# Attention scores from fp16 halves, one exponential per tile, and splits moved to GpSimd

## The chip, the core and the metric

The kernel runs on one core of one Trainium2 chip. A core has TensorE (PE), VectorE (DVE), ScalarE (ACT), GpSimd (POOL) and SyncE (SP), which each take their own instructions in order and meet through semaphores. The metric is the device time of one execution in microseconds; lower is better. Times of one instruction come from one profiled execution.

## What is computed

The reference is one transformer layer on 2048 tokens of width 256: a layer norm, attention with 16 heads of 128, an output projection, a layer norm and a residual; then a mixture of 8 small experts of which the router picks 2 per token, again with norms and a residual. The weights of attention are codes times a scale for each block of 32 rows. What matters here, cut:

```python
q = _mxfp4_matmul(x, wq_codes, wq_scales) + bq      # likewise k, v
scores = jnp.einsum('bqhd,bkhd->bhqk', q, k) / jnp.sqrt(jnp.float32(HEAD_DIM))
attn = jax.nn.softmax(scores, axis=-1)
out = jnp.einsum('bhqk,bkhd->bqhd', attn, v).reshape(B, S, NUM_HEADS * HEAD_DIM)
return _mxfp4_matmul(out, wo_codes, wo_scales) + bo
```

## The kernel before

The kernel keeps nearly fp32 precision by cutting numbers in two parts, a high and a low one, and multiplying high by high, high by low and low by high. Each product of 128 x 128 by 128 x 512 therefore costs three matmuls.

It has three stages: a prologue (layer norm of x, transposed and cut into two fp16 parts; the first weights; the first Q and K), the attention loop, and a tail (output projection, norms, router, experts). The instruction order is written by hand: the program fixes the order on each engine, and a tile layer only adds the semaphore waits that the use of tiles and buffers asks for.

The attention loop (L611 to L665) runs over 256 steps g; a step is one head h and one tile t of 128 queries against all 2048 keys. In a step, in program order:

- `scores_half` (L382) for keys 0 to 1023: six matmuls into a PSUM buffer of 128 x 1024 fp32 (L388, L389, L392), from Q and K held as two fp32r parts; then VectorE takes the row maximum (L393). The PSUM pool has three such buffers, each a tile of its own.
- `recip` of the step before (L413, L416), `flush` (which issues VectorE work left pending by the projections), and one `pv_unit`: six matmuls (L455 to L457) of probabilities times V, for a block of four tiles that lies 13 units back.
- `high_part` of the step before (L420): ScalarE scales the fp32 probabilities p to fp16 (ph), and SP issues a DMA that transposes ph into the tile PT.
- `scores_half` for keys 1024 to 2047, `negmax` (L399), and `softmax` (L406): two exponentials of 1024 columns, one for each half's buffer, each with a row sum.
- another `pv_unit`; then `low_part` of the step before: p times the reciprocal minus ph, 1536 columns on VectorE (L432) and 512 on GpSimd (L438, L439), and its DMA transpose (L440).
- `fill` (L472): a piece of the projections for coming steps, four matmuls of 512 columns (Q or K, L187) or of 256 (V, L206). ScalarE writes the high part (L193, L216), and VectorE the low part (L194, L217), both out of PSUM; the next piece uses the same PSUM buffer "pj".

After eight units a block's result leaves PSUM in two fp16 parts (L463 on ScalarE, L464 on VectorE) and goes to memory by a DMA from GpSimd's queue (L467). SP issues all transposes, in program order: high, low, high, low.

In the prologue V's weights are divided by a power of two found from their largest scale: a maximum on VectorE, an all-reduce over partitions on GpSimd (L341), and a few VectorE steps. Q's and K's weights have a fixed factor.

The lines that the exponential's structure rests on:

```python
s = psS.tile([128, 2, 512], F32, name="s")          # L385, pool of 3
nc.scalar.activation(                               # L406, for each half
    p[:, bass.ts(half, 1024)], ss[half].rearrange("p a b -> p (a b)"),
    AF.Exp, bias=m[:, 2:3], scale=ISQ, accum_out=m[:, 3 + half : 4 + half],
)
```

## Time and profile before

| | |
|---|---|
| time, three runs | 1897.87 us median (1895.89 to 1903.79) |
| the profiled execution: span | 1897.5 us |
| its mean granted TensorE clock | 0.994 |
| attention loop, first to last L399 | 42.4 to 1601.4 us |
| TensorE busy (matmul) | 1832.9 us, 97% |
| VectorE busy | 1640.9 us, 86% |
| ScalarE busy | 1328.2 us, 70% |
| GpSimd busy | 883.7 us, 47% |
| DMA transposes | 2 x 256, 4.0 to 4.1 us from issue to landing |

Times are microseconds from the span's start. PE is TensorE's matmul, PEld its weight load, which runs beside it. Matmuls are pipelined and their ends are modelled, so a busy TensorE is not a TensorE at its rate: the distance from one matmul's start to the next tells that. A group's row gives the line, the engine, the operation, what is written from what, the shape and the count; then busy us in total and mean ns of one; then the idle time of the engine ahead of it and what ended most of that. "issue" is waiting for which the profile shows no releaser.

### The profile page before, as it was taken

To read this page: it belongs to the slowest core of one execution; us is meant where nothing else is said; L and a number is where in the kernel's file an instruction comes from. 1 tells how busy PE (TensorE), PEld (TensorE's weight loads), DVE (VectorE), ACT (ScalarE), POOL (GpSimd) and SP (SyncE) were. 2 spreads that over 40 slices of the span, in tenths; PEclk is the share of its full clock that TensorE was granted. 3 is DMA by queue.
4 is the path that set the end of the run, shared out by engine and by line. 5 is a ranking of instruction groups with operands and counts; after the bars stand their busy time and mean duration, and the time that the engine had idled before them with its cause. 6 is when DMAs were issued, how large, how long until landed. Compare 5 with 4: busy or idle time off the path is not lost.

```text
span 1897.5 us, 25913 instructions
## 1 busy us (share of the span) xinstructions
PE 1832.9 (97%) x8886; PEld 1161.5 (61%) x8886; DVE 1640.9 (86%) x2293; ACT 1328.2 (70%) x1730; POOL 883.7 (47%) x732
## 2 busy tenths in 40 slices
PE   5899999999999999999999999999999999899998
PEld 3555556555565565655655556655556555588887
DVE  5999998999999999999999999999999987468566
ACT  4877788778787778787878788777878777123232
POOL 2853465445444554455445544554444565233222
PEclk8999999999999999999999999999999999999999
DMA  2999999999999998899989988999899999982121
GB/s 75 192 188 179 179 207 184 188 184 194 192 184 182 208 202 186 183 193 204 183 174 199 205 180 187 190 210 185 181 186 192 222 222 243 257 250 70 51 68 56
DMA packets 1147220, 342.20 MB, mean 180 GB/s; under 512 B 1077008, under 2 KB 1137328, under 8 KB 1147088
## 3 DMA queue, kind: packets, MB, share of 16 engines
q1 hardware_dynamic: 1139152, 321.57, 81.9%
q0 software_dynamic: 5216, 16.81, 3.7%
q10 hardware_dynamic: 2720, 2.17, 0.4%
q8 instruction: 70, 1.15, 0.3%
q14 instruction: 62, 0.51, 0.1%
HBM read 53.08 MB, written 18.94 MB: 38 GB/s over the span
## 4 chain that ended last, share of the span: by engine, by line
PE 48%; DVE 9%; ACT 4%; DMA 4%; issue 3%; SPq 1%; POOL 0%; ACTq 0%; DVEq 0%; POOLq 0%
PE s L389 6%; PE s L388 6%; PE s L392 6%; PE pv L455 6%; PE pv L456 6%; PE pv L457 6%; PE gup L845 5%; DVE pl L432 4%; DMA pt<-pl 3%; PE pj L187 3%; ACT ph L420 3%; DVE m L393 2%; PE dps L884 2%; PE pj L206 1%; PE op L690 1%
## 5 line engine op out<-in xcount | busy, mean ns | idle before, releaser
L420 ACT ACTIVATE ph<-p,m 128x2048 f16<-128x2048 f32 x256 | 512.6, 2003 | 240.3 <-issue 134.9
L393 DVE TENSOR_REDUCE m<-s 128x1 f32<-128x1024 f32 x512 | 623.2, 1217 | 60.9 <-PE s L392 58.1
L406 ACT ACTIVATE p<-s,m 128x1024 f32<-128x1024 f32 x512 | 565.3, 1110 | 80.6 <-DVE m L399 76.4
L432 DVE SCALAR_TENSOR_TENSOR pl<-p,m,ph 128x1536 f16<-128x1536 f32 (+1 forms) x256 | 575.8, 2249 | 47.1 <-ACT ph L420 21.1
L439 POOL TENSOR_TENSOR pl<-pr,ph 128x512 f16<-128x512 f32 x262 | 486.5, 1857 | 264.7 <-issue 142.2
L388 PE MATMUL s<-kT,qT 128*128 128x512 f32 x1024 | 485.1, 474 | 5.3 <-ACT p L406 5.3
L389 PE MATMUL s<-kT,qT 128*128 128x512 f32 x1024 | 403.8, 394 | 0.0
L455 PE MATMUL pv<-pt,v 128*128 128x512 f16 x1024 | 393.4, 384 | 2.2 <-DVE o L464 2.0
L456 PE MATMUL pv<-pt,v 128*128 128x512 f16 x1024 | 388.7, 380 | 2.9 <-DMA pt<-pl 1.7
L457 PE MATMUL pv<-pt,v 128*128 128x512 f16 x1024 | 388.6, 379 | 0.0
L438 POOL TENSOR_SCALAR pr<-p,m 128x512 f32<-128x512 f32 x262 | 187.3, 715 | 329.5 <-DVE m L416 307.1
L392 PE MATMUL s<-kT,qT 128*128 128x512 f32 x1024 | 317.2, 391 | 0.0
L388 PEld LDWEIGHTS s<-kT,qT 128*128 128x128 f32 x1024 | 193.3, 189 | 79.0 <-ACT p L406 10.1
L392 PEld LDWEIGHTS s<-kT,qT 128*128 128x128 f32 x1024 | 192.2, 188 | 45.1
L389 PEld LDWEIGHTS s<-kT,qT 128*128 128x128 f32 x1024 | 193.5, 189 | 33.3
L455 PEld LDWEIGHTS <-v 128*128 128x128 f16 x1024 | 99.4, 97 | 185.7 <-issue 116.5
L457 PEld LDWEIGHTS <-v 128*128 128x128 f16 x1024 | 100.3, 98 | 121.2 <-issue 1.5
L456 PEld LDWEIGHTS <-v 128*128 128x128 f16 x1024 | 101.2, 99 | 75.3 <-issue 4.7
L859 POOL TENSOR_TENSOR hh<-sg,hh 128x512 fp32r<-128x512 f32 x42 | 54.5, 1299 | 143.6 <-ACT hh L858 106.6
L467 POOL DMA_DIRECT2D ot_d<-o x63 | 37.2, 590 | 172.8 <-DVE o L464 172.7
L858 ACT CAST hh<-sg 128x512 fp32r<-128x512 f32 (+1 forms) x45 | 27.5, 611 | 116.0 <-DVE sg L870 115.9
L406 ACT ACTIVATION_READ_ACCUMULATOR p<-s,m 128x1 f32 x512 | 99.7, 195 | 0.0
(160 smaller groups left out, 1727.5 us busy)
## 6 DMA issues: line engine op xcount, KB each, us to landing
oi<-ot_d SPq DMA_DIRECT2D x32, 512.0 KB, 5.9
ot_d<-o POOLq DMA_DIRECT2D x63, 256.0 KB, 5.4
pt<-ph SPq DMA_TRANSPOSE x256, 4.1
pt<-pl SPq DMA_TRANSPOSE x256, 4.0
cu<-ct_d SPq DMA_DIRECT2D x16, 256.0 KB, 3.7
xt<-in_L_attn_x SPq DMA_DIRECT2D x4, 512.0 KB, 5.2
wos<-in_L_attn_wo_scales ACTq DMA_DIRECT2D x32, 64.0 KB, 4.2
woc<-in_L_attn_wo_codes SPq DMA_DIRECT2D x8, 256.0 KB, 3.4
```

The lines of the kernel that those rows point to most:

```text
L388: nc.tensor.matmul(s[:, j, :], q[:, 0, qc], k[:, 0, :], start=True, stop=False)
L389: nc.tensor.matmul(s[:, j, :], q[:, 0, qc], k[:, 1, :], start=False, stop=False)
L392: nc.tensor.matmul(s[:, j, :], q[:, 1, qc], k[:, 0, :], start=False, stop=True)
L393: nc.vector.tensor_reduce(m[:, half : half + 1], s.rearrange("p a b -> p (a b)"), AX.X, ALU.max)
L406: nc.scalar.activation(p[:, bass.ts(half, 1024)], ss[half].rearrange("p a b -> p (a b)"), AF.Exp, bias=m[:, 2:3], scale=ISQ, accum_out=m[: ...
L420: nc.scalar.activation(ph, p, AF.Copy, scale=m[:, 6:7])
L432: nc.vector.scalar_tensor_tensor(pl[:, :cv], p[:, :cv], m[:, 6:7], ph[:, :cv], ALU.mult, ALU.subtract)
L438: nc.gpsimd.tensor_scalar(pr, p[:, cs], m[:, 6:7], 1.0, ALU.mult, ALU.mult)
L439: nc.gpsimd.tensor_tensor(pl[:, cs], pr, ph[:, cs], ALU.subtract)
L455: nc.tensor.matmul(ps, vh, d[:, :, c, :], start=(c == 0), stop=False)
L456: nc.tensor.matmul(ps, vh, d[:, :, 16 + c, :], start=False, stop=False)
L457: nc.tensor.matmul(ps, vl, d[:, :, c, :], start=False, stop=(c == 15))
```

## The change

- **Scores.** Q and K become two fp16 parts in place of two fp32r parts. The weights of Q, K and V are each divided by a power of two found from the largest scale and bias; the product of the powers goes into the exponential's scale, which is now read from memory. The powers come from a chain of two PE transposes, one small matmul and VectorE steps in the prologue, in place of the all-reduce.
- **One exponential.** The three PSUM score buffers become one tile `s6` of three slots of 1024 columns. A tile's two halves take the next two slots, and one instruction makes the exponential over both; where the slots are 2 and 0 the halves are exchanged. A small ScalarE copy scales the row sum, and `recip` is one instruction.
- **Splits on GpSimd.** In the loop, ScalarE evacuates a projection's PSUM (Q, K and V) to an fp32 tile `t32`, and GpSimd makes both fp16 parts from it. The block results of P.V go the same way.
- **Low part on VectorE.** `low_part` becomes two calls of `low_half` of 1024 columns: the first at the end of the step in which `high_part` ran, the second a step later, after the next first reduce. The low part's transpose is issued with the second.
- **Prologue.** The start is put in another order around the new scales, and its PSUM tiles come from `s6` too. Buffers of the tail move (the tile `at`, the load of one block).

The core of the diff; prologue order, renamed operands and comments are cut:

```diff
     def scale_s(which):
-        f = sig[:, 1:2] if which == "v" else 1.0 / XS
+        f = sig[:, 2, IX[which] : IX[which] + 1]
         ps, sc, cd = raw[(0, which)]
...
-    psS = ctx.enter_context(tc.tile_pool(name="psS", bufs=3, space=PSUM))
     psA = ctx.enter_context(tc.tile_pool(name="psA", bufs=1, space=PSUM))
+    s6_ctx = ExitStack()
+    s6 = s6_ctx.enter_context(tc.tile_pool(name="ps6", bufs=1, space=PSUM)).tile(
+        [128, 3, 1024], F32, name="s"
+    )
+    slots = [0]
+
+    def s_slot():
+        slots[0] += 1
+        return (slots[0] - 1) % 3
+
+    def s_pair():
+        return s6[:, s_slot()].rearrange("p (a b) -> p a b", a=2)
+
...
     def proj_psum(tag):
         if tag == "s":
-            return psS.tile([128, 2, 512], F32, name="pjs", tag="s", bufs=3)[:, 0]
+            return s_pair()[:, 0]
...
-    def proj_qk(which, h, b, tag="pj"):
+    def proj_qk(which, h, b, tag="pj", wide=None):
         w = W[(h // 2, which)]
-        bias = (bqT if which == "q" else bkT)[:, h : h + 1]
+        bias = bqs[:, IX[which], h : h + 1]
...
-        t = kqv.tile([128, 2, 512], F32R, name=which + "T", bufs=8 if which == "k" else 2)
-        nc.scalar.activation(t[:, 0, :], ps, AF.Identity, bias=bias)
-        pending.append(lambda: nc.vector.scalar_tensor_tensor(
-            t[:, 1, :], ps, bias, t[:, 0, :].bitcast(F32), ALU.add, ALU.subtract
-        ))
+        t = kqv.tile([128, 2, 512], HP, name=which + "T", bufs=8 if which == "k" else 2)
+        if wide is None:
+            nc.scalar.activation(t[:, 0, :], ps, AF.Identity, bias=bias)
+            pending.append(lambda: nc.vector.scalar_tensor_tensor(
+                t[:, 1, :], ps, bias, t[:, 0, :], ALU.add, ALU.subtract
+            ))
+        else:
+            t32 = wide.tile([128, 512], F32, name="t32")
+            nc.scalar.activation(t32, ps, AF.Identity, bias=bias)
+            nc.gpsimd.tensor_copy(t[:, 0, :], t32)
+            nc.gpsimd.tensor_tensor(t[:, 1, :], t32, t[:, 0, :], ALU.subtract)
...
+        if wide is None:
+            nc.scalar.copy(v[:, 0, sl, :], psv)
+            pending.append(lambda: nc.vector.tensor_tensor(
+                v[:, 1, sl, :], psv, v[:, 0, sl, :], ALU.subtract
+            ))
+        else:
+            t32 = wide.tile([128, 512], F32, name="t32")[:, : n * 256].rearrange(
+                "p (t d) -> p t d", d=256
+            )
+            nc.scalar.copy(t32, psv)
+            nc.gpsimd.tensor_copy(v[:, 0, sl, :], t32)
+            nc.gpsimd.tensor_tensor(v[:, 1, sl, :], t32, v[:, 0, sl, :], ALU.subtract)
...
-        smax = st.tile([128, 128], F32, bufs=1)
+        smax = st.tile([128, 3, 128], F32, bufs=1)
+        b48 = st.tile([48, 128], F32, bufs=1)
...
+        for i, scales in enumerate((wq_scales, wk_scales, wv_scales)):
+            nc.scalar.dma_start(
+                out=smax[:, i], in_=scales.rearrange("b (c n) -> (b c) n", n=128)
+            )
+        for i, bias in enumerate((bq, bk, bv)):
+            nc.scalar.dma_start(
+                out=b48[16 * i : 16 * i + 16], in_=bias.rearrange("(h p) -> h p", p=128)
+            )
...
+        def sig_rows():
+            ps = psA.tile([128, 512], F32, name="smt", tag="pj")
+            nc.tensor.transpose(ps[:3, :128], sm[:, 0:3], ident)
+            sgp["t"] = ps
+
+        def sig_pow():
+            nc.vector.tensor_reduce(t3[:, 0:1], sgp["t"][:3, :128], AX.X, ALU.max)
+            nc.vector.tensor_scalar(t3[:, 1:2], t3[:, 0:1], 1e-30, None, ALU.max)
+            nc.vector.tensor_scalar(
+                t3.bitcast(I32)[:, 2:3], t3.bitcast(I32)[:, 1:2], 0x7F800000, None,
+                ALU.bitwise_and,
+            )
+            nc.vector.tensor_scalar(t3[:, 3:6], ident[:3, :3], t3[:, 2:3], None, ALU.mult)
+            ps = psA.tile([128, 512], F32, name="sgb", tag="pj")
+            nc.tensor.matmul(ps[:, :3], one3, t3[:, 3:6], start=True, stop=True)
+            sgp["s"] = ps
+
+        def sig_all():
+            nc.vector.tensor_scalar(sig[:, 0], sgp["s"][:, :3], 0.125, None, ALU.mult)
+            nc.vector.reciprocal(sig[:, 1], sig[:, 0])
+            nc.vector.tensor_scalar(sig[:, 2], sig[:, 1], 1.0 / XS, None, ALU.mult)
+
...

     def scores_half(h, t, half, m):
         q = Q[(h, t // 4)]
         qc = bass.ts(t % 4, 128)
-        s = psS.tile([128, 2, 512], F32, name="s")
+        slot = s_slot()
+        s = s6[:, slot].rearrange("p (a b) -> p a b", a=2)
         for j in range(2):
...
             nc.tensor.matmul(s[:, j, :], q[:, 1, qc], k[:, 0, :], start=False, stop=True)
-        nc.vector.tensor_reduce(
-            m[:, half : half + 1], s.rearrange("p a b -> p (a b)"), AX.X, ALU.max
-        )
-        return s
+        nc.vector.tensor_reduce(m[:, half : half + 1], s6[:, slot], AX.X, ALU.max)
+        return slot

     def negmax(m):
         nc.vector.tensor_scalar(
-            m[:, 2:3], m[:, 0:1], m[:, 1:2], -ISQ, ALU.max, ALU.mult
-        )
-
-    def softmax(h, t, ss, m):
+            m[:, 2:3], m[:, 0:1], m[:, 1:2], ssc[:, 1:2], ALU.max, ALU.mult
+        )
+
+    def softmax(slot0, slot1, m):
         p = soft.tile([128, S], F32, name="p")
-        for half in range(2):
-            nc.scalar.activation(
-                p[:, bass.ts(half, 1024)], ss[half].rearrange("p a b -> p (a b)"),
-                AF.Exp, bias=m[:, 2:3], scale=ISQ, accum_out=m[:, 3 + half : 4 + half],
-            )
+        src = s6[:, slot0 : slot1 + 1 : slot1 - slot0]
+        nc.scalar.activation(
+            p.rearrange("p (a b) -> p a b", a=2), src,
+            AF.Exp, bias=m[:, 2:3], scale=ssc[:, 0:1], accum_out=m[:, 3:4],
+        )
+        nc.scalar.activation(m[:, 4:5], m[:, 3:4], AF.Copy, scale=1.0 / PS)
         return p

     def recip(m):
-        nc.vector.tensor_scalar(
-            m[:, 5:6], m[:, 3:4], m[:, 4:5], 1.0 / PS, ALU.add, ALU.mult
-        )
-        nc.vector.reciprocal(m[:, 6:7], m[:, 5:6])
+        nc.vector.reciprocal(m[:, 6:7], m[:, 4:5])

     def high_part(h, t, m, p):
...
+        if half == 0:
+            LOW[(h, t)] = soft.tile([128, S], HP, name="pl")
+        pl = LOW[(h, t)]
+        cs = bass.ts(half, 1024)
         nc.vector.scalar_tensor_tensor(
-            pl[:, :cv], p[:, :cv], m[:, 6:7], ph[:, :cv], ALU.mult, ALU.subtract
-        )
-        for c in range(cv, S, POOL_COLS):
-            cs = slice(c, c + POOL_COLS)
-            pr = soft.tile([128, POOL_COLS], F32, name="pr", bufs=1)
-            nc.gpsimd.tensor_scalar(pr, p[:, cs], m[:, 6:7], 1.0, ALU.mult, ALU.mult)
-            nc.gpsimd.tensor_tensor(pl[:, cs], pr, ph[:, cs], ALU.subtract)
-        nc.sync.dma_start_transpose(
-            out=PT[(h, t // 4)][:, t % 4, 16:32, :], in_=pl
-        )
+            pl[:, cs], p[:, cs], m[:, 6:7], ph[:, cs], ALU.mult, ALU.subtract
+        )
+        if half == 1:
+            nc.sync.dma_start_transpose(
+                out=PT[(h, t // 4)][:, t % 4, 16:32, :], in_=LOW.pop((h, t))
+            )

     pvps = {}
...
@@ -458,12 +527,16 @@
         if c1 == 16:
             if (h, b) == (NH - 1, 3):
                 o = kqv.tile([128, 2, 512], HP, name="o_last", tag="v", bufs=7)
+                nc.scalar.activation(o[:, 0, :], ps, AF.Copy, scale=1.0 / PS)
+                nc.vector.scalar_tensor_tensor(
+                    o[:, 1, :], ps, 1.0 / PS, o[:, 0, :], ALU.mult, ALU.subtract
+                )
             else:
                 o = soft.tile([128, 2, 512], HP, name="o", bufs=1)
-            nc.scalar.activation(o[:, 0, :], ps, AF.Copy, scale=1.0 / PS)
-            nc.vector.scalar_tensor_tensor(
-                o[:, 1, :], ps, 1.0 / PS, o[:, 0, :], ALU.mult, ALU.subtract
-            )
+                t32 = soft.tile([128, 512], F32, name="t32")
+                nc.scalar.activation(t32, ps, AF.Copy, scale=1.0 / PS)
+                nc.gpsimd.tensor_copy(o[:, 0, :], t32)
+                nc.gpsimd.tensor_tensor(o[:, 1, :], t32, o[:, 0, :], ALU.subtract)
             nc.gpsimd.dma_start(out=ot_d[b][:, h], in_=o)
...
@@ -615,31 +687,36 @@
             if t in (0, 3, 6) and h % 2 == 0 and h + 2 < NH:
                 load_w(h // 2 + 1, "vkq"[t // 3], stage, nc.sync)
             m = small.tile([128, 8], F32, name="m", bufs=6)
-            s0 = scores_half(h, t, 0, m)
+            order = (1, 0) if slots[0] % 3 == 2 else (0, 1)
+            s0 = scores_half(h, t, order[0], m)
             if g == 0:
                 proj_v(0, 0, 2)
                 proj_v(0, 2, 2, "pv")
         if g == NS:
+            load_oi(0, 1, 1)
             load_oi(0, 1, 2)
             load_oi(0, 1, 3)
         if prev is not None:
             recip(prev[2])
+        if prev2 is not None:
+            low_half(1, *prev2)
+        if prev is not None:
+            prev = (*prev, high_part(*prev))
         flush()
         if defer:
             pv_unit(2 * g - 1)
             defer = False
         pv_unit(2 * g)
+        if live:
+            s1 = scores_half(h, t, order[1], m)
+            negmax(m)
+            p = softmax(min(s0, s1), max(s0, s1), m)
         if prev is not None:
-            hl = high_part(*prev)
-        if live:
-            s1 = scores_half(h, t, 1, m)
-            negmax(m)
-            p = softmax(h, t, (s0, s1), m)
+            low_half(0, *prev)
+        prev2 = prev
         first = live and (2 * g + 1 - PVLAG) % 8 == 0
         if not first:
             pv_unit(2 * g + 1)
-        if prev is not None:
-            low_part(*prev, hl)
         if live:
             fill(h, t)
...
     UEND = 2 * (NS + 2)
-
-    # -------------------------------------------------------------------- tail
+    s6_ctx.close()
+    psS = ctx.enter_context(tc.tile_pool(name="psS", bufs=3, space=PSUM))
```

## The prediction

> **What bounds the kernel now.** I read the page's busy shares first, then the stretch between the first and the last of the 256 steps, then a few steps row by row, then the groups by shape. The page:

> ```profile
> span 1897.5 us, 25913 instructions
> ## 1 busy us (share of the span) xinstructions
> PE 1832.9 (97%) x8886; PEld 1161.5 (61%) x8886; DVE 1640.9 (86%) x2293; ACT 1328.2 (70%) x1730; POOL 883.7 (47%) x732
> ```

> TensorE looks full and VectorE nearly so. L399 runs once a step; its view gives 256 starts from 42.4 to 1601.4 us, so a step takes 1559.0 / 255 = 6.11 us, and attention is 82% of the span. Its stretch (columns: busy us of each engine, granted clock, DMA share, GB/s):

> ```profile
> 42.40:1601.40 1559.00, 1531.53 (x7052) 916.60 (x7051) 1439.59 (x1827) 1235.39 (x1576) 787.80 (x647) 1.00 0.96 193
> ```

> Whether TensorE is at its rate is told by the distance between matmul starts (timeline: start us, us, engine, line):

> ```profile
> 799.82 0.39 PE L392 MATMUL s<-kT,qT 128*128 128x512 f32 x1
> ...
> 800.25 1.22 DVE L393 TENSOR_REDUCE m<-s 128x1 f32<-128x1024 f32 x1 [0.22 <-PE s L392]
> ...
> 801.50 0.21 DVE L399 TENSOR_SCALAR m<-m 128x1 f32<-128x1 f32 x1
> ...
> 801.84 1.12 ACT L406 ACTIVATE p<-s,m 128x1024 f32<-128x1024 f32 x1
> ...
> 802.68 0.39 PE L388 MATMUL s<-kT,qT 128*128 128x512 f32 x1
> ...
> 802.91 0.39 PE L389 MATMUL s<-kT,qT 128*128 128x512 f32 x1
> ...
> 803.60 0.39 PE L455 MATMUL pv<-pt,v 128*128 128x512 f16 x1
> 803.61 0.10 PEld L456 LDWEIGHTS <-v 128*128 128x128 f16 x1
> 803.83 0.38 PE L456 MATMUL pv<-pt,v 128*128 128x512 f16 x1
> ```

> A row lasts 0.39 us, but the next begins after 0.23 (fp32r scores) or 0.216 (fp16). A step has 12 score matmuls (12 x 0.231 = 2.77), 12 for P.V (12 x 0.216 = 2.59) and, on average, two 512-wide and two 256-wide ones of the projections (2 x 0.216 + 2 x 0.109 = 0.65): 6.01 of 6.11 us. So TensorE bounds the step, and only 0.10 us of it is waiting. The same rows give the handovers that I need: last score matmul's start to the reduce 0.43 us (799.82 to 800.25); reduce end to L399 0.035; L399's end to the exponential 0.12.

> ```profile
> L393 DVE TENSOR_REDUCE m<-s 128x1 f32<-128x1024 f32 x512 | 623.2, 1217 | 60.9 <-PE s L392 58.1
> L432 DVE SCALAR_TENSOR_TENSOR pl<-p,m,ph 128x1536 f16<-128x1536 f32 x250 | 566.2, 2265 | 46.5 <-ACT ph L420 20.5 <-DMA pt<-pl 19.4 <-ACT p L406 1.3
> L406 ACT ACTIVATE p<-s,m 128x1024 f32<-128x1024 f32 x512 | 565.3, 1110 | 80.6 <-DVE m L399 76.4 <-POOL pr L438 1.1 <-PE pj L206 0.3
> L420 ACT ACTIVATE ph<-p,m 128x2048 f16<-128x2048 f32 x256 | 512.6, 2003 | 240.3 <-issue 134.9 <-DVE m L416 38.1 <-ACT kT L193 29.8
> L439 POOL TENSOR_TENSOR pl<-pr,ph 128x512 f16<-128x512 f32 x262 | 486.5, 1857 | 264.7 <-issue 142.2 <-ACT ph L420 58.9 <-DMA pt<-pl 46.0
> ```

> **The change, part by part.**

> *Scores in fp16.* 12 x (0.231 - 0.216) = 0.18 us of TensorE a step, 46 us over 255, if TensorE stays the bound: 5.83 us a step.

> *Splits on GpSimd, low part on VectorE.* VectorE per step becomes two reduces 2.43, L399's successor 0.21, the reciprocal 0.16, two low halves of 1.28 (shortest of the six 128x1024 rows of L432; their mean of 1.59 holds collisions), gaps 0.18: 5.54 us. It loses L413 (0.20), the Q/K and V splits and the output split. ScalarE: exponential 2.1, a [128,1] copy of about 0.2, high part 2.0, evacuations (0.68 + 0.37)/2 + 0.60/4: about 5.0. GpSimd: a 512 cast at 0.69 (L438, one input, 512 elements) and a subtraction at 1.16 (L439 left alone) for Q/K, about half for V, the same plus a 0.59 DMA issue every fourth step: about 2.0, where it had 2.6. All lie under 5.83, so by busy sums alone TensorE would keep the bound and gain up to 0.28 x 255 = 72 us. The transposes stay two a step, in the same order on SP (low of one tile, high of the next). The second low half comes half a step later; P.V of a block starts over a step after that, and a transpose lands in 4.0 us, so nothing is late.

> *One PSUM tile for all scores.* This decides. The exponential over two slots needs them in one tile, so the three score buffers become one tile of three slots. The built program lists what each instruction waits for (slot offsets 0, 1024, 2048). For one step it reads

> ```
> PE  first scores matmul, slot 0     waits for ACT: exponential of the step before (slots 1 and 2)
> PE  first scores matmul, slot 1     waits for DVE: this step's reduce of slot 0
> DVE reduce of slot 0                waits for PE: its scores, and ACT: the same exponential
> ```

> and so it goes on through the rotation; in the program before, the first scores matmul of a tile waits for the exponential of that very buffer, three tiles back. None of the new waits is for the slot that is written: writes into the tile wait for its last reader, wherever that read. [...]

> A step then is one serial chain. From the first scores matmul: 5 x 0.216 to the sixth's start, 0.425 to the reduce, 1.215: 2.72. To TensorE 0.06 (L217 ends at 812.93, its waiting L187 load starts at 812.99): second half starts at 2.78. Again 1.08 + 0.425: reduce 4.28 to 5.50; 0.035 + 0.214: 5.75; 0.116: exponential at 5.86. Its cost is not in the trace: L406 (bias from memory) takes 1.11 for 1024 and L420 (scale from memory) 2.00 for 2048. [...] I take 2.04, each end 0.04 x 255 = 10 us away. The accumulator read ends 0.09 later, and TensorE starts 0.05 after that (rows of L388 that waited for ACT): **8.05 us a step**.

> What lies beside it: behind the waiting score matmuls stand P.V and the projections. Between the halves TensorE has one P.V unit (1.30) for 1.48 us, between the steps another and the fill (1.95) for 3.97, so it idles 2.2 us a step and none of its work lengthens the chain. ScalarE's high part waits for the reciprocal (2.92) and runs 3.0 to 5.0, an output evacuation to 5.6, before the exponential at 5.86. VectorE's second low half runs 2.95 to 4.23, just before the reduce at 4.28; there is no room there. The fp16 gain survives only as 10 x 0.015 = 0.15 inside the chain, counted above. DMA asks for less per us than now.

> GpSimd and the low halves exclude each other: L432 at 801.88 takes 2.83 beside L439 where its shortest is 1.81. A Q/K split's subtraction ends at about 2.98 of the next step, right where the low half wants to start, so I add 0.02 a step (5 us). Bounds: nothing (V steps, and a gain is excluded, since the chain has no other member to lose), or, if the cast costs what the one 128x128 cast of L103 did (1.8, itself beside a low part), 1.05 in every other step, 135 us. I take the near end, as all small casts (L104 to L108, 0.21) and L438 fit the price of one input.

> *Prologue and end.* The power-of-two scale now goes through two transposes, a tiny matmul and small VectorE steps instead of the all-reduce on GpSimd (VectorE waited 6.4 us for it), but the Q and K weights wait for it too, behind six small DMAs on ACT's queue (bkT took 7.1 us to land), and the start's PSUM work shares the one tile. -6 to +8; I take 0. The tail only moves buffers: 0, +-2.

> **Sum.** 255 x (8.05 - 6.11) = 494, plus 5: 1897.5 + 499 = 2396, say 2397. The profiled span and the median of the runs (1897.87) differ by 0.4 us, so no correction.

> **Rivals.**
> *The slots behave as three buffers* (the waits are met early or are not kept). The bound is then TensorE at 5.83 with VectorE at 5.54 plus collisions behind it: half of the 72 us, 1860, faster. [...] Against: the listed waits are for the latest instruction, not an old one. It decides from the point where the exponential ends before P.V and fill are through, 1.95 us after the second half; it ends 3.9 after. 4% (1% of that within 0.5%).
> *The shared port stretches the chain:* the dear cast; half-way 2465, at worst 2530. 8%.
> *TensorE's idle lowers its clock:* in the stretch 1612 to 1622, with an idle of 3.7 us, the granted clock was 0.92; after a single idle of 2.03 us (1672.44, L845) it stayed 1.00. The new idle of 2.0 comes every step. At half clock the halves cost 2.2 more: over 2900. 3%.

> **Numbers.** Likeliest, the serial chain at 2397: 85%. Low end: exponential at 2.00 and prologue -6, with 0.03 less for handovers: 2370. High end: some of the port's collisions, 0.2 a step, and the page's 2.08: 2455. A measurement of this kernel can tell 0.5% from no change. Faster 4%, same 1%, slower 95%.

> **What would show it.** In the profile after: step 8.05 us between two L471; TensorE about 75% busy in attention, with two waits a step, for ACT L478 (about 2.0 us) and DVE L467 (about 0.2); L462 to L463 starts 0.216 apart; L478 near 2.04; low halves near 1.28; granted clock 1.00. Steps near 5.9 with no wait for L478 would prove me wrong, as would low halves near 2.3.

## The result and the profile after

The changed kernel takes 2524.9 us (median of 4, 2519.7 to 2528.6) against 1898.3 us before (median of 4): a ratio of 1.330, 95% interval 1.326 to 1.333. The direction and the serial chain were forecast; the time lies 128 us above 2397 and 70 above the range. The page's first lines:

```profile
span 2521.6 us, 25363 instructions
## 1 busy us (share of the span) xinstructions
PE 1960.5 (78%) x8890; PEld 958.8 (38%) x8890; DVE 1553.2 (62%) x2011; ACT 1339.3 (53%) x1474; POOL 675.3 (27%) x788
```

No engine is full any more. VectorE has less to do (1553 us after 1641), GpSimd too (675 after 884), and TensorE has nearly the same number of matmuls (8890 after 8886); its 1960 us, after 1833, hold some at a lower clock. Attention runs from the first L471 at 43.7 to the last at 2233.4 us: 2189.7 / 255 = 8.59 us a step, where it was 6.11. That is +630.7 us of a span grown by 624.1; ahead of it +1.3, behind it -7.9. The stretch of attention (columns: us, busy us of PE, PEld, DVE, ACT, POOL, then the granted clock, DMA share, GB/s) and the rows that the account further below comes back to:

```profile
43.70:2233.40 2189.70, 1661.12 (x7053) 713.90 (x7052) 1351.10 (x1535) 1245.97 (x1321) 581.12 (x704) 0.95 0.73 138
...
L505 DVE SCALAR_TENSOR_TENSOR pl<-p,m,ph 128x1024 f16<-128x1024 f32 x512 | 683.7, 1335 | 3.0 <-DMA pt<-pl 2.1
L478 ACT ACTIVATE p<-s,m,ssc 128x2048 f32<-128x2048 f32 x256 | 526.6, 2057 | 283.8 <-DVE m L471 281.1
L213 POOL CAST qT<-t 128x512 f16<-128x512 f32 x63 | 38.4, 610 | 532.8 <-ACT t L212 532.8
...
L471 DVE TENSOR_SCALAR m<-m,ssc x256: 271/273/275, 43.7 to 2233.4; 128x1 f32<-128x1 f32 x128
```

One step in the timeline (start us, us, engine, line; in brackets the idle time and who ended it):

```profile
1005.26 0.38 PE L462 MATMUL s<-kT,qT 128*128 128x512 f16 x1 [1.71 <-ACT p L478]
1005.48 0.38 PE L463 MATMUL s<-kT,qT 128*128 128x512 f16 x1
...
1006.82 1.22 DVE L467 TENSOR_REDUCE m<-s 128x1 f32<-128x1024 f32 x1 [2.66 <-PE s L466]
...
1008.10 0.38 PE L462 MATMUL s<-kT,qT 128*128 128x512 f16 x1
...
1009.59 1.22 DVE L467 TENSOR_REDUCE m<-s 128x1 f32<-128x1024 f32 x1 [0.29 <-PE s L466]
...
1010.85 0.27 DVE L471 TENSOR_SCALAR m<-m,ssc 128x1 f32<-128x1 f32 x1
...
1011.22 2.06 ACT L478 ACTIVATE p<-s,m,ssc 128x2048 f32<-128x2048 f32 x1 [1.07 <-DVE m L471]
1013.18 0.19 ACT L478 ACTIVATION_READ_ACCUMULATOR p<-s,m,ssc 128x1 f32 x1
...
1013.42 0.38 PE L462 MATMUL s<-kT,qT 128*128 128x512 f16 x1 [2.14 <-ACT p L478]
```

The chain is there link by link: scores, reduce, the second scores only after the reduce has ended (1008.04 to 1008.10), reduce, maximum, exponential, and the next step's scores only 0.05 us after the accumulator read. From 1005.26 to 1013.42 are 8.16 us; 8.05 was forecast. 0.05 of the difference is in the first handover (1.56 from first matmul to reduce, not 1.50), 0.04 in L471 and the way to ScalarE, 0.02 in the exponential.

The starts of L471 lie 8.16 us apart in 174 of the 255 steps, and some 9.60 in most of the 70 that touch a stretch at half clock. Of the profile's 72 records of half clock 70 last 3.413 us, one 6.827, and the one at the program's end 8.806; they begin at multiples of 3.413 us from each other. So here are windows of that length in a row (from:to, us, then the columns of above):

```profile
1009.57:1012.99 3.42, 1.72 (x10) 0.88 (x9) 2.69 (x3) 2.35 (x2) 0.00 (x0) 1.00 0.82 151
1012.99:1016.40 3.41, 2.89 (x13) 1.26 (x13) 1.42 (x3) 0.93 (x5) 1.06 (x2) 1.00 0.01 2
...
1023.23:1026.64 3.41, 3.32 (x17) 1.42 (x15) 3.12 (x4) 2.00 (x1) 1.04 (x1) 1.00 1.11 267
1026.64:1030.05 3.41, 1.27 (x9) 0.71 (x8) 1.97 (x3) 2.47 (x4) 0.00 (x0) 1.00 1.04 193
1030.05:1033.47 3.42, 3.42 (x10) 1.21 (x9) 1.17 (x2) 0.14 (x1) 1.06 (x2) 0.50 0.62 114
```

A window in which TensorE is busy 1.72 us is followed by one at full clock; the window with 1.27 us (37%) is followed by one at 0.50. In that one ten matmul records stand where busy windows at full clock have 16 to 18, the distance of the starts goes from 0.216 to 0.42 or 0.43, and the step takes 1.44 us more:

```profile
1029.75 0.38 PE L462 MATMUL s<-kT,qT 128*128 128x512 f16 x1 [2.13 <-ACT p L478]
...
1030.29 0.63 PE L462 MATMUL s<-kT,qT 128*128 128x512 f16 x1
1030.71 0.63 PE L463 MATMUL s<-kT,qT 128*128 128x512 f16 x1
```

TensorE's idle of 2.13 us follows a piece of V, which is shorter than a piece of Q or K. Here it lies whole in one window. Over the trace such an idle behind a piece of V lay whole in one window at full clock 46 times, and half clock followed every time. Where two windows share it, full clock followed in 46 of 50 cases. The idle of 1.71 us behind a piece of Q or K was followed by full clock in all 63. So in this trace the length of the gap alone does not decide; half clock went with how much of it fell into one window.

Windows at 0.50 come one in ten over most of attention (995.9, 1030.1, 1064.2 us and so on), 75 in the whole span. 255 x (8.59 - 8.16) = 109 us.

### The profile page after: what moved, and what is told of

The parts are those of the page before. It is cut to its first block, busy times and chain, and to the rows that moved or that the text cites. A ratio compares the mean times of both kernels' runs of the same rounds, so it can differ in the third digit from the quotient of the medians.

```text
span 2521.6 us, 25363 instructions
## 1 busy us (share of the span) xinstructions
PE 1960.5 (78%) x8890; PEld 958.8 (38%) x8890; DVE 1553.2 (62%) x2011; ACT 1339.3 (53%) x1474; POOL 675.3 (27%) x788
## 4 chain that ended last, share of the span: by engine, by line
PE 45%; DVE 28%; ACT 22%; issue 3%; DMA 1%; POOL 0%; ACTq 0%; DVEq 0%; SPq 0%; POOLq 0%
ACT p L478 22%; DVE m L467 21%; PE s L462 12%; PE s L466 10%; PE s L463 9%; PE gup L924 4%; DVE m L471 3%; PE pv L524 2%; PE pv L525 2%; PE pv L526 2%; PE dps L963 1%; DVE pl L505 1%; PE op L769 1%; PE op_s L769 1%; DVE at L796 0%
## 5 line engine op out<-in xcount | busy, mean ns | idle before, releaser
L467 DVE TENSOR_REDUCE m<-s 128x1 f32<-128x1024 f32 x512 | 626.9, 1224 | 827.1 <-PE s L466 827.1
L490 ACT ACTIVATE ph<-p,m 128x2048 f16<-128x2048 f32 x256 | 512.6, 2002 | 653.9 <-DVE m L486 651.2
L462 PE MATMUL s<-kT,qT 128*128 128x512 f16 x1024 | 406.1, 397 | 520.2 <-ACT p L478 495.9
L505 DVE SCALAR_TENSOR_TENSOR pl<-p,m,ph 128x1024 f16<-128x1024 f32 x512 | 683.7, 1335 | 3.0 <-DMA pt<-pl 2.1
L478 ACT ACTIVATE p<-s,m,ssc 128x2048 f32<-128x2048 f32 x256 | 526.6, 2057 | 283.8 <-DVE m L471 281.1
L524 PE MATMUL pv<-pt,v 128*128 128x512 f16 x1024 | 414.6, 405 | 6.4 <-ACT t L537 6.0
L463 PE MATMUL s<-kT,qT 128*128 128x512 f16 x1024 | 413.2, 404 | 0.0
L525 PE MATMUL pv<-pt,v 128*128 128x512 f16 x1024 | 407.3, 398 | 2.6 <-DMA pt<-pl 2.6
L526 PE MATMUL pv<-pt,v 128*128 128x512 f16 x1024 | 402.2, 393 | 0.0
L463 PEld LDWEIGHTS <-qT 128*128 128x128 f16 x1024 | 101.6, 99 | 708.0 <-issue 644.0
L466 PE MATMUL s<-kT,qT 128*128 128x512 f16 x1024 | 336.6, 413 | 0.0
L244 POOL CAST v<-t 128x256 f16<-128x256 f32 (+1 forms) x105 | 43.1, 410 | 596.8 <-ACT t L243 596.8
L213 POOL CAST qT<-t 128x512 f16<-128x512 f32 x63 | 38.4, 610 | 532.8 <-ACT t L212 532.8
L525 PEld LDWEIGHTS <-v 128*128 128x128 f16 x1024 | 105.9, 103 | 157.3 <-issue 52.9
L524 PEld LDWEIGHTS <-v 128*128 128x128 f16 x1024 | 106.6, 104 | 142.0 <-issue 36.6
L466 PEld LDWEIGHTS <-qT 128*128 128x128 f16 x1024 | 106.7, 104 | 141.3 <-issue 33.0
L526 PEld LDWEIGHTS <-v 128*128 128x128 f16 x1024 | 104.6, 102 | 134.4 <-issue 29.1
L462 PEld LDWEIGHTS <-qT 128*128 128x128 f16 x1024 | 100.4, 98 | 114.7 <-issue 8.7
L538 POOL CAST o<-t 128x512 f16<-128x512 f32 x63 | 38.5, 612 | 342.9 <-ACT t L537 342.9
L539 POOL TENSOR_TENSOR o<-t,o 128x512 f16<-128x512 f32 x63 | 102.1, 1620 | 5.1
```

Source lines behind the costliest of these rows:

```text
L462: nc.tensor.matmul(s[:, j, :], q[:, 0, qc], k[:, 0, :], start=True, stop=False)
L463: nc.tensor.matmul(s[:, j, :], q[:, 0, qc], k[:, 1, :], start=False, stop=False)
L466: nc.tensor.matmul(s[:, j, :], q[:, 1, qc], k[:, 0, :], start=False, stop=True)
L467: nc.vector.tensor_reduce(m[:, half : half + 1], s6[:, slot], AX.X, ALU.max)
L478: nc.scalar.activation(p.rearrange("p (a b) -> p a b", a=2), src, AF.Exp, bias=m[:, 2:3], scale=ssc[:, 0:1], accum_out=m[:, 3:4],)
L490: nc.scalar.activation(ph, p, AF.Copy, scale=m[:, 6:7])
```

## The experiments

The three things to tell apart are the waits of the shared tile, the links of the chain, and the clock. "Clean step" below is the length of most steps with no half-clock window in them; the mean is over all 255. Each ratio is to the kernel before, timed beside that run. The runs came in three groups, beside which the kernel before took 1902.7, 1892.5 and 1890.8 us: between runs of different groups some 10 us mean little. The unused slot, the late high part, the loads at 0, 4, 8 and the splits back are the second group; the constants and the last three runs are the third.

### The waits

**Three tiles again.** All of the change stays but the shared tile and the single exponential.

```diff
-    s6 = ... .tile([128, 3, 1024], F32, name="s")      # one tile, three slots
+    ps3 = ... tile_pool(name="ps6", bufs=3, space=PSUM)  # s = ps3.tile([128, 2, 512], F32)
-        nc.scalar.activation(p, src, AF.Exp, ...)       # 2048 columns
+        for half, s in enumerate((s0, s1)):             # 1024 columns each
```

> The changed kernel with one thing undone: three separate score tiles of 1024 columns and two exponentials of 1024 a step, as before the change; fp16 parts, GpSimd splits and low halves stay. Theory (the shared tile's waits chain TensorE, the reduces and the exponential): TensorE bounds the step again, 12 x 0.216 + 12 x 0.216 + 0.65 = 5.83 us of it and some 0.05 of gaps, so 2521.6 - (2189.7 - 255 x 5.88) = 1831 us, 1820 to 1870, and the granted clock is 1.0 in all of attention. Rival (the splits, the low halves or their port collisions are what stretches the step): still over 2400 us.

Measured: 1944.1 us, 1.023 [1.020, 1.025] of before: 581 us below the changed kernel. The page:

```profile
PE 1805.5 (93%) x8890; PEld 940.1 (48%) x8890; DVE 1612.3 (83%) x2267; ACT 1371.5 (71%) x1730; POOL 902.7 (46%) x788
...
L518 PE MATMUL pv<-pt,v 128*128 128x512 f16 x1024 | 391.9, 383 | 73.3 <-ACT t L531 70.0
L454 PE MATMUL s<-kT,qT 128*128 128x512 f16 x1024 | 392.1, 383 | 22.6 <-ACT p L470 22.6
```

TensorE's waiting for the exponential falls from 495.9 us to 22.6, so the theory holds against its rival. But 1944 is 113 above what I worked out, and the clock is not full in all of attention as expected (0.99 on average). Steps of 5.82 to 5.84 are there as forecast, yet about every fourth takes 6.78, and even heads have several of 7 to 10 us; the first row of L518 names a new wait. These are followed further below.

**The kernel before, with its score buffers made slots of one tile.** Nothing else is changed.

> The kernel before with one thing changed: the three score tiles are slots of one tile; two exponentials a step, fp32 parts and whole low part as before. Theory: the same chain, longer by 0.16 for the wider matmul spacing (0.231) and some 0.1 to 0.2 for the second exponential, shorter by 0.06 for the plain scalar in the row maximum, about 8.4 us a step, and cold windows of 0.4 a step: 1898 + 255 x (8.8 - 6.11) = 2585 us, 2500 to 2650. Rival (the waits cost little by themselves; the new work costs the time): under 2000 us.

Measured: 2690.4 us, 1.414 [1.410, 1.418]. The sharing alone makes the old kernel as slow as that, so neither the splits nor the low halves are needed to explain the loss. The size was missed, 40 us above the range: the clean step is 8.69, not 8.4, which I did not follow further, and the mean is 9.23, with 114 windows at half clock.

**The third slot left unused in attention.** `slot = half` in place of the rotation.

> The changed kernel with the third score slot left unused in attention: the first half of every step goes to slot 0, the second to slot 1 of the same tile. Theory (every write into the tile waits for the tile's last reader, whichever slot it read): the third slot does nothing, each step takes 8.16 us as before and 9.60 where a window is at half clock; 2525 us, 2515 to 2535. Rival (the third slot lets some scores run beside the exponential): the first half now has to wait for what it did not wait for, 1.3 us a step at most, over 2600 us.

Measured: 2527.4 us, 1.337 [1.333, 1.341]; the clean step is 8.16, the mean 8.59, as in the changed kernel. The wait of TensorE for the exponential, first in this kernel and then in the changed one (us in total, times, longest):

```profile
PE s L462 <- ACT p L478: 496.0, 255, 3.9
```

```profile
PE s L462 <- ACT p L478: 495.9, 255, 3.9
```

A third of the score space can be taken away and the time stays. That is the plainest sign that waits are for the tile and not for the slot: the third slot holds data, but no work runs beside other work because of it.

### The links of the chain

**Two exponentials over the shared tile.** One of 1024 columns for each slot, and the row sum added as before.

> The changed kernel with two exponentials of 1024 columns over the slots of the shared tile in place of one of 2048, and the two small additions for the row sum. Theory: the exponential lies on the chain, so its second fixed cost (0.1 to 0.25 us) comes on top of each step: 2525 + 255 x 0.2 = 2576 us, 2545 to 2600; this is then what the single exponential saves on this chain. Rival (TensorE waits for the last read only and the two halves pipeline with the accumulator reads): within 10 us of 2525.

Measured: 2730.4 us, 1.435 [1.430, 1.439], 205 us above the changed kernel and far from the 2576 expected. The clean step is 8.49. The pair, in the timeline:

```profile
1003.08 1.20 ACT L478 ACTIVATE p<-s,m,ssc 128x1024 f32<-128x1024 f32 x1 [1.10 <-DVE m L471]
1004.18 0.19 ACT L478 ACTIVATION_READ_ACCUMULATOR p<-s,m,ssc 128x1 f32 x1
1004.28 1.19 ACT L478 ACTIVATE p<-s,m,ssc 128x1024 f32<-128x1024 f32 x1
1005.37 0.20 ACT L478 ACTIVATION_READ_ACCUMULATOR p<-s,m,ssc 128x1 f32 x1
```

From 1003.08 to 1005.57 are 2.49 us where the single one with its read takes 2.15 (1011.22 to 1013.37): 0.34, or 85 us over 255 steps. The other 120 us are clock: 162 windows at 0.50 in place of 75, and a mean step of 9.41, 0.91 above the clean one. The idle behind a piece of Q or K is 2.04 us here, where it was 1.71, and all 36 that lie whole in one window are now followed by half clock. So on this chain the single exponential is worth 0.33 us a step, and the clock charged more than that on top. Beside the three-tile kernel, which also makes two exponentials, this run shows that the shared tile costs the time, and not their number.

**Constants for the two scalars from memory.** The row maximum takes `-ISQ` and the exponential `scale=ISQ`; the power-of-two factors of Q and K are left out.

> The changed kernel with constants in place of the two scalars read from memory in the row maximum and in the exponential; this leaves the range scale of Q and K out of the softmax, so the output is another. Theory (both lie on the chain): the row maximum falls from 0.273 to 0.214 us, the exponential by 0.09 (two halves took 1.20 each with the scalar from memory, 1.11 before the change), so a step falls from 8.16 to 8.01: 2525 - 255 x 0.15 = 2487 us, 2470 to 2495. Rival (the steps are held by something beside this chain): 2525 us.

Measured: 2512.9 us, 1.331 [1.327, 1.335]. L471 in its own view (ns: shortest, median, longest):

```profile
L471 DVE TENSOR_SCALAR m<-m x256: 212/214/216, 44.4 to 2217.4; 128x1 f32<-128x1 f32 x128
```

and L478 among the groups:

```profile
L478 ACT ACTIVATE p<-s,m 128x2048 f32<-128x2048 f32 x256 | 503.6, 1967 | 292.3 <-DVE m L471 289.7 <-PE pj L224 2.6
```

The clean step is 8.01, to the hundredth what the two links give: 0.059 from L471 (0.273 before) and 0.090 from L478 (2.057). Yet the time falls by 12 us and not by 38, and beside the kernel before the ratio is no better (1.331 after 1.330). The mean step is 8.52, as 95 windows are at half clock in place of 75; the mean granted clock of the four runs is 0.933 to 0.940, where the changed kernel had 0.948 to 0.951. The idle behind a piece of V, now 1.98 us, lay whole in one window 59 times, where it was 46, and half clock followed 57 times. Both theories miss the time; the first has the step right.

### The clock

**More TensorE work in the idle time.** The projection matmuls of attention are issued twice (Q, K) or up to three times (V) into the same PSUM buffer.

> The changed kernel with the matmuls of every projection step in attention issued twice (Q, K) or three times (V), so 0.86 us more of TensorE work in each step, in the idle time of 1.7 to 2.1 us ahead of the first scores; the result is the same. Theory (a window of 3.413 us in which TensorE streams less than about 0.365 of the time is followed by one at half clock): the windows at half clock go, every step takes 8.16 us, and the time is 2525 - 108 = 2417 us, 2405 to 2435. Rival (the stretched steps have another cause, or the clock falls by a timetable of its own): 2525 us or more.

Measured: 2455.6 us, 1.293 [1.289, 1.296]: 69 us less with 1332 matmuls more. Attention as a whole and three windows, with the columns of above:

```profile
43.96:2159.08 2115.12, 1773.97 (x8385) 823.05 (x8383) 1342.53 (x1536) 1245.97 (x1321) 598.14 (x704) 0.99 0.76 143
...
1006.16:1009.57 3.41, 2.15 (x15) 1.25 (x13) 1.07 (x1) 2.58 (x4) 0.65 (x2) 1.00 0.60 111
...
1023.23:1026.64 3.41, 2.15 (x12) 0.92 (x10) 0.75 (x2) 1.83 (x4) 1.06 (x2) 1.00 1.16 212
1026.64:1030.05 3.41, 3.32 (x16) 1.41 (x15) 3.12 (x4) 2.00 (x1) 0.00 (x0) 1.00 0.36 66
```

The emptiest of these windows now hold 2.15 us of TensorE, and in heads 1 to 13 nearly every step is 8.16. The clock therefore follows the load here, not a timetable, and the stretched steps were its work. The gain is 39 us less than expected: attention still holds 34 us above 8.16 a step, 21 of them in heads 14 and 15, which have few projections to repeat or none (steps of up to 10.89 us); 26 windows at 0.50 remain.

### What keeps the rest from being faster

The three-tile kernel has the changed arithmetic and the old overlap, and is still 2.3% slower than before. In its timeline, around the step of 6.78 us:

```profile
548.22 2.00 ACT L484 ACTIVATE ph<-p,m 128x2048 f16<-128x2048 f32 x1 [0.27 <-ACT t L236]
...
550.13 0.58 ACT L531 ACTIVATE t<-pv 128x512 f32<-128x512 f32 x1
...
550.76 0.38 PE L518 MATMUL pv<-pt,v 128*128 128x512 f16 x1 [0.78 <-ACT t L531]
```

The change moved `high_part` ahead of the first P.V unit. Its 2.00 us now stand in ScalarE's queue before the evacuation of the finished block, and TensorE waits to reuse that PSUM buffer (0.78 us here). In the changed kernel the chain hid it: TensorE waited there for that evacuation 6.0 us in all, where it is 70.0 here.

**High part back behind the P.V unit.** Only the two lines are exchanged.

> The kernel with three separate score tiles and two exponentials (1944 us), with the high part's instruction back behind the first P V unit of the step, as it stood before the change. Theory: in every fourth step, one of 6.78 us among steps of 5.83, the last P V unit's evacuation on ScalarE stood behind the 2.00 us of the high part, and TensorE waited for it; now it stands ahead of it: 64 x 0.95 = 61 us less, 1883 us, 1870 to 1900. Rival (the evacuation is late for another reason): 1944 us.

Measured: 1905.0 us, 1.007 [1.005, 1.010]: 39 us of the 61 by the times, 29 by the ratios. An odd head goes from 97.0 to 94.3, but the fourth step only from 6.78 to 6.29.

**Weight loads at steps 0, 4, 8.** On top of the run before.

> As the run before (three tiles, two exponentials, high part behind the P V unit), with the weight loads of the even heads issued at steps 0, 4 and 8 in place of 0, 3 and 6, and their dequantization at steps 2, 6 and 10. Theory: on SP's queue a weight load waited for GpSimd to release the staging buffer and held the transposes behind it, two stalls of 2.5 to 4.5 us in each of the heads 2 to 12 (an even head takes 104.7 us, an odd one 97.0): 6 x 7.7 = 46 us less than the run before, 1837 us, 1825 to 1860, and every step at 5.8 to 5.9. Rival (the stalls come from the low halves' own order): unchanged against the run before.

Measured: 1884.7 us, 0.997 [0.995, 0.998]: 20 us of the 46. Even heads still take 98 to 101 us. P.V now waits for the low part's transpose (the waits between 200 and 1500 us: total, times, longest):

```profile
DVE pl L499 <- DMA pt<-pl: 31.8, 22, 3.2
PE pv L519 <- DMA pt<-pl: 30.3, 18, 2.5
```

So the queue behind a waiting load was at most part of it.

**The splits back on ScalarE and VectorE.** On top of the run with the loads at 0, 4, 8.

> As the run before, with the splits of Q, K, V and the head outputs back on ScalarE and VectorE (high part by ScalarE from PSUM, low part by VectorE from PSUM), so that GpSimd only dequantizes. Theory: VectorE takes 113 x 0.44 + 127 x 0.73 + 63 x 0.69 = 186 us more, beside 1612 us that it has, 98% of an 1837 us run: it becomes the bound in some steps, 1837 + 60 = 1897 us, 1860 to 1950. Rival (VectorE's slack in each step, 0.9 us, takes it): within 10 us of the run before.

Measured: 1960.2 us, 1.037 [1.034, 1.040]. Steps of 5.98 to 6.58 stand where 5.65 to 6.29 stood; beside the run before, GpSimd's splits save 75 us. On three tiles, with the low part on VectorE, this part of the change is a gain; in the changed kernel the chain sets the step and hides it.

**The low part in one instruction; the loads on ScalarE's queue; both.** Each on top of the run with the loads at 0, 4, 8.

> As the kernel with three tiles, high part late and loads later (1885 us), with the low part of a tile in one VectorE instruction of 2048 columns, where its first half stood. Theory: VectorE still fits into the step (0.27 + 2.5 + 1.22 + 0.36 + 1.22 = 5.6 of 5.8 us), and the low part's transpose leaves half a step earlier, so P V waits less for it in the even heads: 1870 us, 1855 to 1885. Rival (the halves are needed to let the reduces through): each reduce of a first half is 1.3 us later and steps grow, over 1900 us.

> As the kernel with three tiles, high part late and loads later (1885 us), with the weight loads of the even heads issued from ScalarE's queue in place of SP's. Theory (the stalls left in the heads 2 to 12, 99.8 us against 94.3, come from the transposes queued on SP behind the loads): 6 x 5 = 30 us less, 1857 us, 1845 to 1870. Rival (the loads share the DMA engines with the transposes, or wait on ScalarE for the staging buffer): 1880 us or more.

> The two edits before together. Theory: with the low part whole its transpose is earlier, with the loads off SP nothing stands ahead of it: heads 2 to 12 at 95 us each, 1850 us, 1840 to 1870. Rival (either edit costs a stall elsewhere): no faster than the better of the two.

Measured: 1880.6 us (0.995 [0.993, 0.997]), 1882.0 us (0.996 [0.995, 0.997]) and 1874.5 us (0.992 [0.990, 0.994]). With the low part whole, most steps are 5.92, and the halves were not needed. That time lies in the range, but P.V's waits for the low part's transpose only fell from 30.3 to 24.8 us, so the reason given for the gain is not shown. The loads alone brought almost nothing, against my theory. Between 200 and 1500 us P.V's waits for that transpose do fall, from the 30.3 us above to 2.5 in 6 waits. But the scores' waits for the exponential rise from 1.9 us in 2 waits to 22.5 in 19. Of the 13 of these that are longer than 0.5 us, 12 come 6 to 8 us after a load was issued from ScalarE's queue. So the stall seems to have moved to ScalarE, as the second half of the rival has it; no run tests that.

Together the two edits give steps of 5.92 with three of 6.65 in most even heads, some 97.3 us, not 95. The last is the fastest kernel here, 0.8% under the one before. It keeps fp16 parts and GpSimd's splits, has the high part back behind the P.V unit and the loads moved, and drops the shared tile, the single exponential and the low halves.

## Where the prediction was right, and which step failed

- **The deciding part, "one PSUM tile for all scores", was right.** The shared tile alone slows the old kernel to 2690 us, its removal brings the new one to 1944, and the third slot is worth nothing. The waits in the built program decide.
- **The chain was mis-sized by 0.11 us a step, 28 us.** "0.035 + 0.214" for the row maximum left out that its scalar now comes from memory (0.273). The 2.04 taken for the exponential was my estimate: no run shows it, nor the 2.08 in the high end of the range; L420, 2048 columns with its scale from memory, has 2.00, and L478 took 2.057. The first handover took 0.05 more than the row of before. By itself this would have left the time inside the range.
- **The step that failed is the clock: "granted clock 1.00" for the likeliest case, with "TensorE's idle lowers its clock" as a rival of 3%.** I gave that rival only as a permanent half clock, "over 2900", because "after a single idle of 2.03 us (1672.44, L845) it stayed 1.00". One idle could not show it: here the idle returns each step, and where 2.13 us of it lie whole in one window of 3.41 us, the 1.27 us of work that are left in it (37%) were followed by a window at 0.50. The gaps are 1.9 us on average (495.9 / 255), and about one window in ten ran at half clock. It cost 109 us, and my range had no room for it: without it the time would have been some 2416 us, inside 2370 to 2455.
- **Smaller terms.** The 5 us for GpSimd beside the low halves did not reach the chain: 174 of the 185 steps clear of half clock take 8.16, and of the 11 longer ones 4 lie in head 0 and 4 in the last two heads. The rows show a low half slowed beside GpSimd (L432 2.83 us beside L439, 1.81 at its shortest); that the two share a port is shown by no run. The small cast took 0.61 us, so the near end was right. The tail was 7.9 us shorter, where 0 +-2 stood, for a reason that was not looked for; the prologue took 1.3 more.
- **The sum.** 28 - 5 + 109 - 8 + 1 = 125 of the 128 us; the profiled span lies 3 us under the median of the runs.
- **The fp16 gain** is there (L462 to L463 0.216), TensorE is 76% busy in attention (75% forecast), and low halves take 1.34 us (1.28).
- **The first rival's 1860** was what a three-buffer version should give. The actual one took 1944, since I had not seen that the high part's move delays P.V's evacuation, nor that the low part's later transpose leaves too little room in even heads. While the chain stood, neither showed.

One exponential over both halves with waits for its own two slots alone was not tried, so what it would give without the chain stays open.

## What to carry to other kernels

Before buffers are merged into one tile to save an instruction, read from the built program what each user of the merged tile will wait for: the 0.33 us a step that one exponential saves here cost over 2 us of overlap. When a change turns a full TensorE into a waiting one, price its clock as well. Here the work in each window of 3.413 us told more than the longest gap, and the shorter chain of the constants (8.01 us a step after 8.16) gave 12 us in place of 38, with 95 windows at half clock in place of 75. And a change that loses as a whole may hold parts that gain: test each on the version without the loss.
